# Four graph layers on one core: the product with v as one operation, the last residual by a transfer, the last five graphs' tiles turned by TensorE

## The chip, the cores and the metric

The kernel runs on one core of a Trainium2 chip. The metric is the time of one execution on the device in microseconds (us), the median of several runs. The engines are named as the profile names them: PE is TensorE's matrix product, PEld its loading of weights, DVE is VectorE, ACT is ScalarE, POOL is GpSimd, and SP is the engine that issues most transfers. PSUM, into which PE writes, is used as eight banks of 128 partitions by 2 KB.

## The reference

64 graphs of 256 nodes with 256 features each go through four layers; each layer's result is added to its input and normalized. All inputs are f32, `adj` is an integer matrix per graph.

```python
x = _layernorm(x + _L0_gnn_ref(x, adj, ...))   # attention with 8 heads of 32, then a feed-forward of 1024
x = _layernorm(x + _L1_gnn_ref(x, adj, ...))   # graph attention: leaky_relu(f_i + f_j), masked, softmax
x = _layernorm(x + _L2_gnn_ref(x, adj, ...))   # the same with another weight, then elu
x = _layernorm(x + _L3_gnn_ref(x, ..., adj, adj))  # two relational convolutions, each with elu
```

What matters here of layers 0 and 3, cut:

```python
# layer 0
scores = einsum('bhqd,bhkd->bhqk', q * scale, k)
attn = softmax(where(allowed, scores, -inf))
ctx = einsum('bhqk,bhkd->bhqd', attn, v)             # the product with v
# layer 3
def conv(x, w_rel, w_root, b):
    out = einsum('bnd,de->bne', x, w_root) + b
    for r in range(R):
        agg = einsum('bij,bid->bjd', masks[r], x) / deg[r]
        out = out + einsum('bjd,de->bje', agg, w_rel[r])
    return out
h = elu(conv(encoded_spans, w_rel1, w_root1, b1))
h = elu(conv(h, w_rel2, w_root2, b2))
return h                                              # then x + h, normalized: the last residual
```

## The kernel before

The kernel is unrolled over the 64 graphs. It first records every operation of every graph with its engine, a cost in microseconds that the author gave it, and the tiles that it reads and writes. A planner (`Plan.schedule`) then lays these operations out in time: on each engine it takes the ready operation that is due first, keeps PE in one mode of array tiling where it can, and gives out buffers from rings of fixed size. The instructions are emitted in that order, and each engine executes its own in order. So a change of one cost, tile or engine can move operations of all graphs.

```python
RINGS = {..., "p": 12, "both": 4, "inv": 1, "ctxT": 2, "X": 8, ..., "o": 4, "blocks": 1, "turned": 1, "xT": 2}
...
class Plan:
    LAG = {"PE": 0.21, "DVE": 0.13, "ACT": 0.13, "POOL": 0.08, "SP": 4.5}
    SWITCH = 0.1          # PE, on a change between "full", "row" and "col"
    PERIOD = 46.0         # a graph is due each 46 us
    LAST, SPACE = 5, 0.1  # the last five graphs are due nearly together
```

A graph has four tiles that must be transposed before they are multiplied with weights: the inputs of the two graph attention layers and of the two convolutions. They are turned through memory: DVE transposes blocks of 32x32, four transfers write the blocks in order to a buffer in HBM, and a fifth reads them back. `transposed` is the other way, used for the feed-forward: TensorE transposes into PSUM and ACT copies the result out.

```python
def transposed(xt):
    xT, pt = new("T", [P, KB, N]), new("bank", [P, KB, N])
    def issue():
        for kb in range(KB):
            for i in range(NB):
                nc.tensor.transpose(pt()[:, kb, i * P : (i + 1) * P], xt()[:, i, kb * P : (kb + 1) * P], ident)
    pe("full", 0.44, issue, [xt], [pt], [xT])
    act(0.47, lambda: nc.scalar.copy(xT(), pt()), [pt], [xT])
    return xT

def bounced(xt):
    turned, rows, xT = new("turned", [P, 4, NB * KB, 32]), new("rows", [P, NB * KB, 4, 32]), new("T", [P, NB * KB, P])
    dve(0.63, lambda: nc.vector.transpose(turned()..., xt()...), [xt], [turned], "uses")      # L629
    for a in range(4):
        op("SP", 0.5, lambda a=a: nc.sync.dma_start(rows()..., turned()...), [turned], [(rows, a)], lag=SENT)   # L633
    op("SP", 0.5, lambda: nc.sync.dma_start(xT()..., rows()...), [rows], [xT], lag=BACK)
    return xT, lambda kb, i: xT()[:, KB * i + kb, :]
```

With the planner's figures `SENT, BACK = 3.0, 4.5` for the time that these transfers take.

The product with v of the attention is done in two halves of four heads (`hg`). Each writes one PSUM bank: the sums of the exponentials and the unnormalized context. DVE takes the reciprocal of the sums and multiplies.

```python
inv = new("inv", [P, KB, N])
for hg in range(KB):
    pc = new("bank", [P, 2, N])
    def values(hg=hg, pc=pc):
        for r in range(4):
            nc.tensor.matmul(pc()[32 * r : 32 * r + 32, 1, :], lhsT=ones, rhs=both[r]()[:, hg, :], start=True, stop=True)   # L771
        for kt in range(NB):
            for r in range(4):
                h = 4 * hg + r
                nc.tensor.matmul(pc()[32 * r : 32 * r + 32, 0, :], lhsT=v()[:, kt, HD * h : HD * (h + 1)],
                                 rhs=p[kt, r]()[:, hg, :], start=(kt == 0), stop=(kt == NB - 1))                            # L776
    pe("col", 1.32, values, [v] + both + list(p.values()), [pc], [ctxT, inv])
    dve(1.62, lambda hg=hg, pc=pc: nc.vector.reciprocal(inv()[:, hg, :], pc()[:, 1, :]), [pc], [(inv, hg)])
    dve(0.28, lambda hg=hg, pc=pc: nc.vector.tensor_tensor(ctxT()[:, hg, :], pc()[:, 0, :], inv()[:, hg, :], op=ALU.mult), ...)
```

A residual is added in one of two ways. `add` is a DVE instruction. `add_later` is a transfer that GpSimd issues and that adds while it writes; so far it serves to add rows of constants to freshly loaded inputs.

```python
def add_later(xt, yt, reads):
    op("POOL", 0.6, lambda: nc.gpsimd.dma_start(xt(), yt(), accum_op=ALU.add), [xt, *reads], [xt], lag=3.0)   # L603
def add(xt, yt):
    dve(0.60, lambda: nc.vector.tensor_tensor(xt(), xt(), yt(), op=ALU.add), [xt, yt], [xt], "uses")          # L609
...
# end of each graph
h = conv(conv(xt, 0, rel, rdeg), 1, rel, rdeg)   # the result is a tile "o"
add(h, xt)                                       # the last residual
layer_norm(h)                                    # DVE statistics (L666, L668), POOL root (L671 to L674), ACT applies (L678)
op("SP", 0.4, lambda: nc.sync.dma_start(out_graph[g], h()), [h], [])
```

Of the kernel before, what the change touches and what calls it, by code (L numbers as in the profile page):

```python
# [17 lines left out]
P = 128  # L18
# [2 lines left out]
BIG = 1e30  # L21
NO_EDGE = -346.0


SENT, BACK = 3.0, 4.5

# [186 lines left out]
def tile_gnn_stack(ctx: ExitStack, tc: tile.TileContext, t: dict, out: bass.AP):  # L213
# [16 lines left out]
    nc = tc.nc  # L230
    x_in, adj_in = t["x"], t["adj"]
    B, N, D = x_in.shape
# [253 lines left out]
    def main_path(plan):  # L486
# [86 lines left out]
        def graph(g):  # L573
# [37 lines left out]
            def transposed(xt):  # L611
# [9 lines left out]
                act(0.47, lambda: nc.scalar.copy(xT(), pt()), [pt], [xT])  # L621
                return xT

            def bounced(xt):

                turned, rows, xT = new("turned", [P, 4, NB * KB, 32]), new("rows", [P, NB * KB, 4, 32]), new("T", [P, NB * KB, P])
                dve(0.63, lambda: nc.vector.transpose(turned().rearrange("p b q n -> p (b q n)"),  # L629
                                                      xt().rearrange("p i (k b c) -> p b (i k) c", k=KB, b=4)),  # L630
                    [xt], [turned], "uses")
                for a in range(4):
                    op("SP", 0.5, lambda a=a: nc.sync.dma_start(  # L633
                        rows().rearrange("(c b) q a n -> c (b q) a n", b=4)[:, :, a, :],
                        turned()[32 * a : 32 * a + 32].rearrange("c b q n -> c (b q) n")), [turned], [(rows, a)], lag=SENT)
                op("SP", 0.5, lambda: nc.sync.dma_start(xT().rearrange("p q n -> p (q n)"), rows().rearrange("p q a n -> p (q a n)")),
                   [rows], [xT], lag=BACK)
                return xT, lambda kb, i: xT()[:, KB * i + kb, :]
# [96 lines left out]
            def attention(xT, am):  # L735

                qk, v = projections(xT)
                ctxT = new("ctxT", [P, KB, N])  # L740
                p = {}
                for kt in range(NB):
                    s = [new("bank", [P, KB, N]) for r in range(4)]
                    for r in range(4):
                        p[kt, r] = new("p", [P, KB, N])

                    def scores(kt=kt, s=s):
                        for hg in range(KB):
                            for r in range(4):
                                f = slice(32 * r, 32 * r + 32)  # L750
                                nc.tensor.matmul(s[r]()[:, hg, :], lhsT=qk()[f, KB + hg, kt * P : (kt + 1) * P],  # L751
                                                 rhs=qk()[f, hg, :], start=True, stop=True)

                    pe("row", 0.97, scores, [qk], s, [p[kt, r] for r in range(4)])
                    for r in range(4):
                        pr, k = p[kt, r], 8 * g + 4 * kt + r
                        act(0.58, lambda pr=pr, k=k, sr=s[r]: nc.scalar.activation(  # L757
                            pr(), sr(), AF.Exp, accum_out=seen_sum[:, k : k + 1]), [s[r]], [pr])
                        dve(0.60, lambda pr=pr, kt=kt: nc.vector.tensor_tensor(  # L759
                            pr(), pr(), am()[:, kt, None, :].to_broadcast([P, KB, N]), op=ALU.mult), [pr, am], [pr], "uses")  # L760
                both = [new("both", [P, KB, N]) for r in range(4)]
                for r in range(4):
                    dve(0.60, lambda r=r: nc.vector.tensor_tensor(both[r](), p[0, r](), p[1, r](), op=ALU.add),  # L763
                        [p[0, r], p[1, r]], [both[r]], "uses")
                inv = new("inv", [P, KB, N])
                for hg in range(KB):
                    pc = new("bank", [P, 2, N])

                    def values(hg=hg, pc=pc):
                        for r in range(4):  # L770
                            nc.tensor.matmul(pc()[32 * r : 32 * r + 32, 1, :], lhsT=ones, rhs=both[r]()[:, hg, :],  # L771
                                             start=True, stop=True)
                        for kt in range(NB):
                            for r in range(4):
                                h = 4 * hg + r
                                nc.tensor.matmul(pc()[32 * r : 32 * r + 32, 0, :], lhsT=v()[:, kt, HD * h : HD * (h + 1)],  # L776
                                                 rhs=p[kt, r]()[:, hg, :], start=(kt == 0), stop=(kt == NB - 1))

                    pe("col", 1.32, values, [v] + both + list(p.values()), [pc], [ctxT, inv])
                    dve(1.62, lambda hg=hg, pc=pc: nc.vector.reciprocal(inv()[:, hg, :], pc()[:, 1, :]), [pc], [(inv, hg)])  # L780
                    dve(0.28, lambda hg=hg, pc=pc: nc.vector.tensor_tensor(
                        ctxT()[:, hg, :], pc()[:, 0, :], inv()[:, hg, :], op=ALU.mult), [pc, (inv, hg)], [(ctxT, hg)])
                act(0.62, lambda: nc.scalar.activation(inv(), inv(), AF.Identity, accum_out=seen_inv[:, g : g + 1]), [inv], [inv])  # L783
                return ctxT
# [32 lines left out]
                return y  # L817

            def gat(xt, layer, gm, seen, bias, finish):
                xT, xT_at = bounced(xt)  # L820
                w, c_w = gw[layer], c_gw[layer]
                h, e, z = new("h", [P, NB, HW]), tok("e"), tok("X")
                for i in range(NB):
                    ph = new("bank", [P, D + 2])
                    pe("full", 0.87, lambda i=i, ph=ph: product(ph(), lambda kb: xT_at(kb, i),
                                                                lambda kb: w[:, kb, :], KB), [xT, c_w], [ph], [h])
                    if bias is None:
                        act(0.27, lambda i=i, ph=ph: nc.scalar.copy(h()[:, i, 0 : D + 2], ph()), [ph], [(h, i)])
                    else:
                        dve(0.34, lambda i=i, ph=ph: nc.vector.tensor_tensor(h()[:, i, 0 : D + 2], ph(), bias, op=ALU.add),  # L830
                            [ph], [(h, i)])
                dve(0.07, lambda: nc.vector.memset(h()[:, :, ONE : ONE + 1], 1.0), [(h, 0), (h, 1)], [(h, "one")])
                dve(0.07, lambda: nc.vector.tensor_tensor(seen_fg[:, seen], h()[:, :, F_COL : G_COL + 1],
                                                          h()[:, :, F_COL : G_COL + 1], op=ALU.mult), [(h, 0), (h, 1)], [], "uses")
                pf = new("bank", [P, N])

                def spread():
                    for i in range(NB):
                        nc.tensor.transpose(pf()[:, i * P : (i + 1) * P],  # L839
                                            h()[:, i, F_COL : F_COL + 1].to_broadcast([P, P]), ident)  # L840

                pe("full", 0.22, spread, [(h, 0), (h, 1)], [pf], [e])
                for i in range(NB):
                    dve(0.40, lambda i=i: nc.vector.scalar_tensor_tensor(e()[:, i, :], pf(), h()[:, i, G_COL : G_COL + 1],  # L844
                                                                         gm()[:, i, :], op0=ALU.add, op1=ALU.min),
                        [pf, (h, i), gm], [(e, i)])
                dve(0.60, lambda: nc.vector.scalar_tensor_tensor(e(), e(), SLOPE, e(), op0=ALU.mult, op1=ALU.max), [e], [e],
                    "uses")
                act(0.52, lambda: nc.scalar.activation(e(), e(), AF.Exp), [e], [e])  # L849
                for i in range(NB):  # L850
                    po, r = new("bank", [P, HW]), new("r", [P, 1])
                    pe("full", 0.87, lambda i=i, po=po: product(po(), lambda kt: e()[:, kt, i * P : (i + 1) * P],
                                                                lambda kt: h()[:, kt, :], NB), [e, h], [po], [z, r])
                    dve(0.08, lambda po=po, r=r: nc.vector.reciprocal(r(), po()[:, ONE : ONE + 1]), [po], [r])
                    finish(i, z, po, r)
                return z
# [37 lines left out]
            def conv(h, layer, rel, rdeg):  # L894
# [1 line left out]


                w, c_w, bias = conv_w[layer], c_cw[layer], conv_b[layer]
                hT, hT_at = bounced(h)
                o, hi, lo, n = tok("o"), new("hi", [P, NB, D + 2], F32R), tok("lo", F32R), tok("e")  # L900
                cols = D if layer else D + 2
                for i in range(NB):
# [47 lines left out]
            rel = relation(load("adj", adj_graph[g], I32))  # L950
            rdeg = new("rdeg", [P, NB])
            h = conv(conv(xt, 0, rel, rdeg), 1, rel, rdeg)
            add(h, xt)
            layer_norm(h)
            op("SP", 0.4, lambda: nc.sync.dma_start(out_graph[g], h()), [h], [])

# [266 lines left out]
```

## Time and profile before

| What | Value |
|---|---|
| Time, median of 3 runs | 2896.01 us (2893.25 to 2898.55) |
| Span of the profiled execution | 2897.1 us |
| L609, DVE, last residual, 128x512 | 64 times, 682 ns each |
| L629, DVE, turning a tile, 128x512 | 256 times for these tiles, 702 to 703 ns each |
| Transfers rows<-turned, T<-rows | 1024 of 64 KB, 2.2 us from issue to landing; 256 of 256 KB, 2.8 us |
| L618, PE, one f32 transpose of 128x128 | 256 times, 277 ns each |
| L621, ACT, copy of 128x512 out of PSUM | 64 times, 588 ns each |
| L771 and L776, PE, product with v | 90.2 and 139.6 us busy |
| L603, POOL, issue of an adding transfer | 128 times, 1278 and 1301 ns each |

In the profile, `out<-in` are the tiles that an instruction writes and reads, by the names in the program. Many operations pass through helpers and so have the helper's line: L657 is the matrix product of every layer. "Idle before" is the time for which an engine stood still before an instruction, with the work that ended the wait. PE's busy time counts matmuls, whose ends are modelled. Time that an engine stands idle costs something only where it lies on the chain of work that sets the end.

### The profile page before, as it was taken

The page shows a single profiled execution, that of the slowest core. Times are in us where ns is not written, and L with a number is a line of the kernel's source. Part 1 is how long each engine was busy: PE and PEld are TensorE (multiplying, and loading weights), DVE is VectorE, ACT ScalarE, POOL GpSimd, SP SyncE. Part 2 cuts the span into 40 slices and gives each one's busy share as a digit, 9 for nine tenths or more (in the row PEclk, how much of TensorE's full clock was granted, in tenths as well). Part 3 has the DMA queues.
Part 4 walks back from the last instruction along what each step waited for, and adds up shares of the span by engine and source line. Part 5 has one row for each costly group of instructions (what it writes and reads, how often), then busy time and mean ns, then how long its engine had stood idle before and what let it go on. Part 6 is the DMA issues. An engine that isn't in the chain of part 4 may idle for free.

```text
span 2897.1 us, 50588 instructions
## 1 busy us (share of the span) xinstructions
PE 2805.3 (97%) x16182; PEld 2128.1 (73%) x16182; DVE 2523.0 (87%) x6557; ACT 1540.4 (53%) x3713; POOL 789.1 (27%) x1685
## 2 busy tenths in 40 slices
PE   8999999999999999999999999999999999999975
PEld 6776777777777767777777777777777777777853
DVE  6879899989989898999889898899888998999686
ACT  3555555546455555655555465555555655555343
POOL 2232223222223222222222322232231332222221
PEclk9999999999999999999999999999999999999998
DMA  7454455445444444454444544444444544443342
GB/s 183 81 108 88 99 101 102 89 101 102 95 92 100 87 94 94 98 101 93 104 97 93 98 99 99 100 91 102 86 93 96 109 88 93 105 90 72 67 83 70
DMA packets 844512, 278.32 MB, mean 96 GB/s; under 512 B 692656, under 2 KB 810672, under 8 KB 844240
## 3 DMA queue, kind: packets, MB, share of 16 engines
q1 hardware_dynamic: 808800, 240.27, 37.7%
q0 software_dynamic: 35440, 34.76, 8.5%
q8 instruction: 131, 2.15, 0.3%
q14 instruction: 141, 1.16, 0.1%
HBM read 157.43 MB, written 83.89 MB: 83 GB/s over the span
## 4 chain that ended last, share of the span: by engine, by line
PE 82%; DVE 10%; ACT 3%; DMA 2%; issue 2%; POOL 1%; SPq 1%; DVEq 0%; POOLq 0%; ACTq 0%
PE bank L657 67%; PE bank L919 4%; PE bank L776 3%; PE bank L751 3%; PE bank L771 2%; DMA rows<-turned 2%; DVE p L759 1%; PE bank L618 1%; DVE turned L629 1%; PE bank L839 1%; SPq L633 1%; DVE st L666 1%; DVE o L929 1%; DVE both L763 1%; DVE e L844 1%
## 5 line engine op out<-in xcount | busy, mean ns | idle before, releaser
L671 POOL TENSOR_SCALAR rstd<-mv 128x2 f32<-128x2 f32 x384 | 104.4, 272 | 1869.8 <-DVE mv L668 1496.7
L678 ACT ACTIVATE X<-X,rstd 128x256 f32<-128x256 f32 x640 | 349.8, 597 | 244.7 <-POOL rstd L674 230.1
L657 PE MATMUL bank<-cw,T 128*128 128x512 f32 x1024 | 467.9, 600 | 9.6 <-DMA T<-rows 9.1
L657 PE MATMUL bank<-T,w 128*128 128x256 f32 x2048 | 471.6, 380 | 5.2 <-ACT p L757 2.6
L657 PE MATMUL bank<-w,hid 128*128 128x256 f32 x2048 | 460.1, 380 | 0.0
L657 PEld LDWEIGHTS bank<-w,hid 128*128 128x128 f32 x2048 | 385.9, 190 | 62.7 <-issue 10.4
L657 PEld LDWEIGHTS bank<-T,w 128*128 128x128 f32 x2048 | 382.7, 190 | 64.5 <-issue 6.9
L757 ACT ACTIVATE p<-bank 128x512 f32<-128x512 f32 x512 | 299.9, 598 | 87.8 <-PE bank L751 87.6
L657 PEld LDWEIGHTS bank<-cw,T 128*128 128x128 f32 x1024 | 192.2, 192 | 209.3 <-issue 195.2
L759 DVE TENSOR_TENSOR p<-p,am 128x512 f32<-128x512 f32 x512 | 332.8, 680 | 10.8 <-ACT p L757 10.7
L672 POOL TENSOR_TENSOR rstd<-rstd,neghalf 128x2 f32<-128x2 f32 x384 | 305.7, 796 | 32.1
L809 ACT ACTIVATE hid<-bank,col_b 128x256 f32<-128x256 f32 x512 | 209.4, 474 | 113.8 <-PE bank L657 112.1
L657 PE MATMUL bank<-xT,wqkv 128*128 128x256 f32 x1024 | 251.6, 387 | 13.4 <-DVE xT L650 12.9
L657 PE MATMUL bank<-h,e 128*128 128x259 f32 x1024 | 253.8, 388 | 11.0 <-ACT e L849 9.3
L657 PE MATMUL bank<-gw,T 128*128 128x258 f32 x1024 | 249.1, 384 | 2.1 <-ACT inv L783 1.5
L657 PEld LDWEIGHTS bank<-h,e 128*128 128x128 f32 x1024 | 192.7, 192 | 66.6 <-issue 19.3
L666 DVE BATCH_NORM_STATS2 st<-X 128x6 f32<-128x256 f32 x640 | 237.5, 413 | 1.8
L906 ACT CAST hi<-bank 128x256 fp32r<-128x256 f32 x256 | 94.6, 370 | 263.4 <-PE bank L657 262.6
L657 PEld LDWEIGHTS bank<-xT,wqkv 128*128 128x128 f32 x1024 | 189.7, 192 | 54.0 <-issue 13.5
L780 DVE RECIPROCAL inv<-bank 128x256 f32<-128x256 f32 x128 | 220.0, 1734 | 8.8 <-PE bank L776 8.6
L657 PEld LDWEIGHTS bank<-gw,T 128*128 128x128 f32 x1024 | 191.1, 191 | 36.7 <-issue 5.2
L629 DVE STREAM_TRANSPOSE turned<-X 128x512 f32<-128x512 f32 x192 | 134.9, 703 | 45.0 <-DMA rows<-turned 23.0
(121 smaller groups left out, 4775.4 us busy)
## 6 DMA issues: line engine op xcount, KB each, us to landing
rows<-turned SPq DMA_DIRECT2D x1024, 64.0 KB, 2.2
T<-rows SPq DMA_DIRECT2D x256, 256.0 KB, 2.8
adj<-in_adj_dram SPq DMA_DIRECT2D x128, 256.0 KB, 3.0
blocks<-in_x_dram SPq DMA_DIRECT2D x512, 32.0 KB, 2.3
x<-in_x_dram SPq DMA_DIRECT2D x64, 256.0 KB, 3.0
xr<-in_x_dram SPq DMA_DIRECT2D x64, 256.0 KB, 2.8
xr<-row_ln_b POOLq DMA_DIRECT2D x64, 256.0 KB, 4.4
x<-row_bo POOLq DMA_DIRECT2D x64, 256.0 KB, 4.8
```

The lines of the kernel that those rows point to most:

```text
L629: dve(0.63, lambda: nc.vector.transpose(turned().rearrange("p b q n -> p (b q n)"), xt().rearrange("p i (k b c) -> p b (i k) c", k=KB, b=4 ...
L657: nc.tensor.matmul(dst, lhsT=lhs(c), rhs=rhs(c), start=(c == 0), stop=(c == n - 1))
L666: nc.vector.bn_stats(stat()[:, i, :], y()[:, i, :])
L671: nc.gpsimd.tensor_scalar(rstd()[:, 0, :], mv()[:, :, 1], 1.0, EPS, op0=ALU.mult, op1=ALU.add)
L672: nc.gpsimd.tensor_tensor(rstd()[:, 0, :], rstd()[:, 0, :], neghalf[:, 0:NB], op=ALU.pow)
L678: nc.scalar.activation(y()[:, i, :], y()[:, i, :], AF.Identity, bias=rstd()[:, 1, i : i + 1], scale=rstd()[:, 0, i : i + 1])
L757: act(0.58, lambda pr=pr, k=k, sr=s[r]: nc.scalar.activation(pr(), sr(), AF.Exp, accum_out=seen_sum[:, k : k + 1]), [s[r]], [pr])
L759: dve(0.60, lambda pr=pr, kt=kt: nc.vector.tensor_tensor(pr(), pr(), am()[:, kt, None, :].to_broadcast([P, KB, N]), op=ALU.mult), [pr, am] ...
L780: dve(1.62, lambda hg=hg, pc=pc: nc.vector.reciprocal(inv()[:, hg, :], pc()[:, 1, :]), [pc], [(inv, hg)])
L809: act(0.36, lambda f=f, k=k, ph=ph: nc.scalar.activation(hid()[:, f + k, :], ph()[:, k, :], AF.Relu, bias=b1[:, f + k : f + k + 1]), [ph, ...
L906: act(0.27, lambda i=i, po=po: nc.scalar.copy(hi()[:, i, 0:D], po()[:, D:]), [po], [(hi, i)])
L919: nc.tensor.matmul(pa()[:, 0:n], lhsT=rel()[:, i, j * P : (j + 1) * P], rhs=part()[:, i, 0:n], start=(c == 0), stop=(c == len(terms) - 1))
```

## The change

Three things are changed. The two halves of the product with v become one operation of the planner, which writes two banks. The last residual is added by a transfer for all graphs but the last two. For the last five graphs (`QUICK`) the four tiles are transposed by TensorE instead of through memory: ACT first copies the tile with its columns rearranged, so that the result has the order of rows that the weights are laid out for. The first is to keep the planner from parting the two halves, the second to take work off DVE, the third to shorten the end, where there are no later graphs to work on meanwhile.

```diff
+QUICK = 5
...
+            def rearranged(xt):
+                if g < B - QUICK:
+                    return bounced(xt)
+                spread = tok("turned")
+                act(0.8, lambda: nc.scalar.copy(spread().rearrange("p i (k c b) -> p (i k) c b", k=KB, b=4),
+                                                xt().rearrange("p i (k b c) -> p (i k) c b", k=KB, b=4)), [xt], [spread])
+                xT = transposed(spread)
+                return xT, lambda kb, i: xT()[:, kb, i * P : (i + 1) * P]
...
                 inv = new("inv", [P, KB, N])
-                for hg in range(KB):
-                    pc = new("bank", [P, 2, N])
-
-                    def values(hg=hg, pc=pc):
+                pcs = [new("bank", [P, 2, N]) for hg in range(KB)]
+
+                def values():
+                    for hg in range(KB):
+                        pc = pcs[hg]()
                         for r in range(4):
...   (the same products, with pc for pc())
-                    pe("col", 1.32, values, [v] + both + list(p.values()), [pc], [ctxT, inv])
+                pe("col", 2.62, values, [v] + both + list(p.values()), pcs, [ctxT, inv])
+                for hg in range(KB):
+                    pc = pcs[hg]
                     dve(1.62, lambda hg=hg, pc=pc: nc.vector.reciprocal(inv()[:, hg, :], pc()[:, 1, :]), [pc], [(inv, hg)])
...
             def gat(xt, layer, gm, seen, bias, finish):
-                xT, xT_at = bounced(xt)
+                xT, xT_at = rearranged(xt)
...   (in conv)
-                hT, hT_at = bounced(h)
+                hT, hT_at = rearranged(h)
...
             h = conv(conv(xt, 0, rel, rdeg), 1, rel, rdeg)
-            add(h, xt)
+            if g < B - 2:
+                add_later(h, xt, [xt])
+            else:
+                add(h, xt)
             layer_norm(h)
```

More of the change, by code (lines that the diff above doesn't have):

```diff
@@ L765, in attention @@
                 inv = new("inv", [P, KB, N])
-                for hg in range(KB):
-                    pc = new("bank", [P, 2, N])
-                    def values(hg=hg, pc=pc):
+                pcs = [new("bank", [P, 2, N]) for hg in range(KB)]
+                def values():
+                    for hg in range(KB):
+                        pc = pcs[hg]()
                         for r in range(4):
-                            nc.tensor.matmul(pc()[32 * r : 32 * r + 32, 1, :], lhsT=ones, rhs=both[r]()[:, hg, :],
+                            nc.tensor.matmul(pc[32 * r : 32 * r + 32, 1, :], lhsT=ones, rhs=both[r]()[:, hg, :],
                                              start=True, stop=True)
@@ L775, in values @@
                                 h = 4 * hg + r
-                                nc.tensor.matmul(pc()[32 * r : 32 * r + 32, 0, :], lhsT=v()[:, kt, HD * h : HD * (h + 1)],
+                                nc.tensor.matmul(pc[32 * r : 32 * r + 32, 0, :], lhsT=v()[:, kt, HD * h : HD * (h + 1)],
                                                  rhs=p[kt, r]()[:, hg, :], start=(kt == 0), stop=(kt == NB - 1))
-                    pe("col", 1.32, values, [v] + both + list(p.values()), [pc], [ctxT, inv])
+                pe("col", 2.62, values, [v] + both + list(p.values()), pcs, [ctxT, inv])
+                for hg in range(KB):
+                    pc = pcs[hg]
                     dve(1.62, lambda hg=hg, pc=pc: nc.vector.reciprocal(inv()[:, hg, :], pc()[:, 1, :]), [pc], [(inv, hg)])
```

## The prediction

> **What bounds the kernel now.** I read the page first (busy times, the span in 40 slices), then busy times by stretch, then the chain that ended last and the waits, both cut to the last 164 us.
>
> The page, engine shares and slices:
>
> ```profile
> PE 2805.3 (97%) x16182; PEld 2128.1 (73%) x16182; DVE 2523.0 (87%) x6557; ACT 1540.4 (53%) x3713; POOL 789.1 (27%) x1685
> ...
> PE   8999999999999999999999999999999999999975
> ...
> DVE  6879899989989898999889898899888998999686
> ...
> PEclk9999999999999999999999999999999999999998
> ```
>
> PE is full in every slice but the first and the last two. DVE is near full too, but with gaps. A number by stretch says more (columns: stretch, its length, busy us and instructions of PE, weight loads, DVE, ACT and POOL, granted clock, DMA share, GB/s):
>
> ```profile
> 40.00:300.00 260.00, 257.36 (x1588) 199.16 (x1587) 224.87 (x558) 140.15 (x352) 67.00 (x142) 1.00 0.50 101
> ...
> 2400.00:2700.00 300.00, 299.16 (x1813) 227.35 (x1812) 273.31 (x683) 168.05 (x414) 76.66 (x174) 1.00 0.42 87
> 2700.00:2733.00 33.00, 33.00 (x157) 29.01 (x156) 15.70 (x41) 12.99 (x30) 8.44 (x19) 1.00 0.33 67
> 2733.00:2780.00 47.00, 37.95 (x166) 30.39 (x165) 37.77 (x123) 17.85 (x37) 13.87 (x35) 0.96 0.40 76
> 2780.00:2840.00 60.00, 48.06 (x161) 28.40 (x160) 48.75 (x158) 24.60 (x53) 10.11 (x28) 0.91 0.44 90
> 2840.00:2897.00 57.00, 30.10 (x94) 15.41 (x92) 31.43 (x89) 19.71 (x38) 6.70 (x20) 0.83 0.25 62
> ```
>
> There are two regimes. From 40 to 2700 us PE is busy 2630 of 2660 us; the nine stretches that I asked for leave it 29.8 us idle together. Nothing done to another engine can bring more than those 29.8 us there. From 2733 us to the end, 164 us, PE is busy 116 us and DVE 118 us: neither is full, and what sets the pace is latency from one engine to the next. In that tail the last graphs have no later graph to hide behind. The chain of work that ended last says the same; its shares by line for 2733 to 2897 us:
>
> ```profile
> by line: PE bank L657 21.3%; issue 6.5%; DMA rows<-turned 6.5%; DVE e L844 4.4%; DVE turned L629 4.4%; DMA T<-rows 4.2%; SPq L633 3.9%; DVE o L929 3.2%; ACT e L934 3.1%; PE bank L919 2.9%; DVE st L666 2.9%; DVE lo L907 2.8%; DVE e L847 2.8%
> ```
>
> The turn of a tile through memory (DVE turned, the issues at SPq L633, both DMAs) is 4.4 + 3.9 + 6.5 + 4.2 = 19.0% of it, 31 us. DVE's turns in this tail are 20, 14 of X and 6 of o; five graphs have 15 and 5, so all but one or two are those of the last five graphs. The timeline of the last one: DVE starts to turn at 2869.97, the product that needs it starts at 2877.73, 7.8 us later. Another, from 2843.47 to 2852.81, took 9.3 us.
>
> **What the Trainium skill says.** "VectorE: DVE Perf Modes", section "The three transpose paths": DVE transposes 32x32 blocks only, TensorE a whole 128x128 into PSUM. That fits this trace: DVE's turn takes 0.70 us and then five transfers have to put the blocks in place. "TensorE: Matmul & The Clock Gate", "Part 4: PE-mode transpose", adds that the result needs a copy out of PSUM; the trace has both, 277 ns for an f32 transpose (L618) and 588 ns for ACT's copy (L621). The same page, "What's actually happening" under the clock gate, says that a TensorE idle for a window of some 3.4 us falls to half clock. The tail agrees: granted clock 0.83 in its last stretch, and the eight products of 128x512 at 2852.81, after 3.05 us of waiting for T<-rows, took 5.37 us where the same eight at 2859.92 took 3.60. "DMA: Bandwidth & Descriptors", "Anatomy of one DMA", puts a transfer from GpSimd at 2.0 us + bytes / 436e3, an estimate of 2.6 us for 256 KB. The trace gives 4.4 and 4.8 us from issue to landing for the same form (xr<-row_ln_b, x<-row_bo), of which 1.26 us is the issuing instruction. The measurement decides.
>
> **Part 1, both halves of the product with v in one operation.** No instruction is added or taken away. The two halves are a burst of 4 + 8 products each, for groups of 32 columns. In the built order before, all 64 graphs already have the two bursts one after the other, with nothing between; so it is after. No change of mode is saved: I count 367 changes before, 371 after. What it changes is planning: two PSUM banks are claimed at once, and the planner lets the first reciprocal (DVE, 1.73 us) follow both bursts instead of the first. On a PE that is full anyway I put this at 0 us.
>
> **Part 2, the last residual by transfer, 62 of 64 graphs.** DVE loses 62 x 0.682 us (row X+o, L609) = 42 us, of its 2523. POOL gains 62 issues x 1.26 us = 78 us on 789. The new wait is at DVE's statistics of o: they cannot start before the sum has landed. The planner believes in 0.6 + 3.0 = 3.6 us for issue and transfer; the rows above measured 4.4 to 4.8. I added up, in the order as built, the DVE work placed between each transfer and its statistics, with the durations of the profile's rows: 4.2 us in the median, 3.8 to 4.5 between the quartiles, 1.2 the least. So DVE, which keeps its order, stands still some 0.2 to 0.6 us in most graphs, 12 to 37 us in all, against 42 us of work saved: about even for DVE, and DVE does not set the end before 2733. For PE I take 0.
>
> **Part 3, the last five graphs turned by TensorE.** Each of 20 turns loses 0.70 us of DVE and five transfers, and gains an ACT copy that rearranges (like other ACT passes over 128x512 from SBUF, 0.63 to 0.72 us), four transposes (0.44 us for the group at 2699.94), and ACT's copy (0.59). With three handovers of 0.05 to 0.2 us that is some 2.1 us in place of 7.8: 5.7 saved per turn on the path. DVE loses 14 us in the tail, ACT gains 20 x 1.3 = 26 on 62, PE 20 x 0.5 = 10 on 116; none gets full by this. On the chain lie 31 / 7.8 = 4 turns, as one would expect of one graph with its two attention layers and two convolutions. So 31 - 4 x 2.1 = 22.6 us leave this chain. Other graphs' chains stand just behind it, waiting for DVE and PE in turn; I let them take back a third and keep 15. The warmer clock may add a little: the 96 products of 128x512 in the tail average 647 ns against 600 over all, 4.5 us, of which I count 1.
>
> **Sum.** Start 0, full stretch 0, tail -16: 2896 - 16 = 2880 us.
>
> **The rivals.** (a) A reshuffle of the full stretch. Parts 1 and 2 alter what the planner sees, and its order changes from the first graphs on: hardly a stretch of PE's order is the same, and from a few graphs on the new order repeats every seven graphs, which the old did not. If that pattern has a place where PE waits, it waits there in every repetition. The stretches before range from 0.5 to 6.3 us of idle per 300, so one like the best all along gives about 20 us more (2860), one with twice the idle costs 30 (2910). Nothing in the profile tells which; it is the largest uncertainty. (b) The transfer stalls DVE more than worked out, because the POOL queue, which waits for o in its order, also holds up the roots of other norms (each waits 1.26 us for an issue where 0.6 was planned), and ACT's longest waits are for just those (L678, 230 us in all). Then DVE and ACT come late by 1 to 2 us per graph. Against it: only 10% of DVE's time is free but PE waits little for DVE now, a few us per line. If a quarter of 62 x 1.5 us reached PE it would be +23: about 2903. (c) The tail's gain is taken back whole, as its other limit is DVE with 118 of 164 us and queues on it: 2896. For this: the chain in the tail also runs through dozens of short DVE pieces. Against it: DVE itself loses 14 us there. (d) All of the 22 us and a warmer clock are kept, and the full stretch loses half its idle: 2858.
>
> **Range and chances.** The tail gives 5 to 25, the full stretch anything from -20 to +20: 2860 to 2902 for 8 times in 10. Two per cent is 58 us; to be under 2838 the kernel would have to lose nearly all idle time of the full stretch and half of the tail's, to be over 2954 it would need about three times the idle of now. Faster by over 2%: 0.03; within: 0.94; slower: 0.03.
>
> **What would show it.** Right: no DVE turned and no rows<-turned in the last 150 us, the stretch after PE ceases to be full some 15 us shorter, clock there at 0.9 or more; DVE about 2470 us busy, with short new waits of st (L666) on the transfer o<-X of 0.2 to 0.6 us each; PE some 2810 us busy, idle between 40 and 2700 us near 30. Wrong: PE idle there of over 45 us with releasers on DVE or POOL (a or b); a tail as long as before with DVE over 80% busy in it (c); or a landing of o<-X well above 4.8 us.

## The result

| | Time, median | Ratio to the kernel before |
|---|---|---|
| Before | 2897.01 us (2893.25 to 2898.55) | |
| Changed | 2866.45 us (2865.78 to 2867.83) | 0.9897 (95% interval 0.9880 to 0.9914) |

The gain is 30 us, within two per cent and within the range that was given, and about twice the 16 us that the sum expected. For experiments the ratio is given with its 95% interval, and "us" is the ratio's distance from 1 times 2897 us.

### The profile page after: what moved, and what is told of

It reads as the page before. It is cut to its first block, busy times and chain, and to the rows that moved or that the text cites. A ratio compares the mean times of both kernels' runs of the same rounds, so it can differ in the third digit from the quotient of the medians.

```text
span 2864.0 us, 50548 instructions
## 1 busy us (share of the span) xinstructions
PE 2799.7 (98%) x16262; PEld 2130.6 (74%) x16262; DVE 2479.8 (87%) x6475; ACT 1563.8 (55%) x3753; POOL 847.5 (30%) x1747
## 3 DMA queue, kind: packets, MB, share of 16 engines
q14 instruction: 139, 1.14, 0.1%
## 4 chain that ended last, share of the span: by engine, by line
PE 72%; DVE 13%; DMA 7%; ACT 2%; issue 2%; SPq 2%; POOL 1%; DVEq 0%; POOLq 0%; ACTq 0%
PE bank L669 59%; DMA o<-X 3%; PE bank L934 3%; PE bank L789 3%; PE bank L763 3%; DMA rows<-turned 2%; DVE p L771 2%; PE bank L784 2%; DVE st L678 1%; SPq L645 1%; DVE turned L641 1%; DVE o L944 1%; PE bank L854 1%; DVE inv L795 1%; PE bank L620 1%
## 5 line engine op out<-in xcount | busy, mean ns | idle before, releaser
L669 PE MATMUL bank<-T,w 128*128 128x256 f32 x2048 | 473.2, 380 | 0.6 <-ACT T L623 0.3
L669 PE MATMUL bank<-cw,T 128*128 128x512 f32 x1024 | 462.7, 595 | 0.6 <-ACT T L623 0.6
L669 PE MATMUL bank<-w,hid 128*128 128x256 f32 x2048 | 459.4, 380 | 0.0
L669 PEld LDWEIGHTS bank<-T,w 128*128 128x128 f32 x2048 | 381.3, 190 | 64.7 <-issue 12.4
L669 PEld LDWEIGHTS bank<-w,hid 128*128 128x128 f32 x2048 | 385.4, 190 | 58.1 <-issue 4.3
L769 ACT ACTIVATE p<-bank 128x512 f32<-128x512 f32 x512 | 299.0, 597 | 75.2 <-PE bank L763 75.1
L669 PEld LDWEIGHTS bank<-cw,T 128*128 128x128 f32 x1024 | 191.5, 190 | 198.9 <-issue 182.0
L669 PE MATMUL bank<-xT,wqkv 128*128 128x256 f32 x1024 | 249.5, 386 | 12.3 <-DVE xT L662 12.3
L669 PE MATMUL bank<-h,e 128*128 128x259 f32 x1024 | 252.2, 386 | 7.4 <-ACT e L864 5.7
L669 PE MATMUL bank<-gw,T 128*128 128x258 f32 x1024 | 249.9, 385 | 7.2 <-DMA T<-rows 2.6
L669 PEld LDWEIGHTS bank<-h,e 128*128 128x128 f32 x1024 | 192.2, 191 | 66.8 <-issue 21.6
L669 PEld LDWEIGHTS bank<-xT,wqkv 128*128 128x128 f32 x1024 | 188.7, 191 | 53.8 <-issue 17.7
L669 PEld LDWEIGHTS bank<-gw,T 128*128 128x128 f32 x1024 | 191.3, 191 | 43.2 <-issue 10.0
L864 ACT ACTIVATE e<-e 128x512 f32<-128x512 f32 x128 | 80.7, 631 | 169.9 <-DVE e L862 169.2
```

The lines of the kernel that those rows point to most:

```text
L669: nc.tensor.matmul(dst, lhsT=lhs(c), rhs=rhs(c), start=(c == 0), stop=(c == n - 1))
L769: act(0.58, lambda pr=pr, k=k, sr=s[r]: nc.scalar.activation(pr(), sr(), AF.Exp, accum_out=seen_sum[:, k : k + 1]), [s[r]], [pr])
```

## The profile after

The page of the changed kernel, engine shares and two of the slices:

```profile
PE 2799.7 (98%) x16262; PEld 2130.6 (74%) x16262; DVE 2479.8 (87%) x6475; ACT 1563.8 (55%) x3753; POOL 847.5 (30%) x1747
...
PE   8999999999999999999999999999999999999987
...
PEclk9999999999999999999999999999999999999999
```

DVE has 82 instructions fewer (62 additions, 20 turns). Their groups are 42.2 and 13.5 us less busy, the 56 us worked out, but the engine as a whole only 43: instructions in a row overlap a little (in the timeline three of 0.68 us take 1.89), and such time counts once. POOL gained 58 us for 62 issues. PE is the surprise: 80 instructions more for the transposes, 12.8 us of busy time, yet 5.6 us less busy in all. The product with v is 6.5 us less busy (85.4 + 137.9 us, before 90.2 + 139.6) and the 128x512 products 5.2; why is not shown. Busy times by stretch (columns as before):

```profile
40.00:2700.00 2660.00, 2635.93 (x15489) 2010.01 (x15489) 2345.63 (x6057) 1453.74 (x3541) 794.28 (x1625) 1.00 0.50 102
...
2733.00:2780.00 47.00, 37.80 (x169) 29.29 (x168) 36.58 (x128) 30.93 (x57) 12.46 (x36) 0.93 0.11 23
2780.00:2820.00 40.00, 38.22 (x163) 24.98 (x162) 32.73 (x114) 28.00 (x53) 6.15 (x16) 1.00 0.10 21
2820.00:2864.00 44.00, 27.74 (x110) 15.79 (x108) 28.47 (x87) 25.72 (x47) 10.91 (x26) 0.90 0.21 56
```

PE is idle 24.1 us between 40 and 2700 us, where it was 29.8. From 2733 us on there are 131 us left instead of 164, with PE busy 104 of them (79%) instead of 116 (71%). The chain that ended last, 2733 to 2864 us:

```profile
by line: PE bank L669 42.8%; DMA o<-X 5.1%; PE bank L934 4.4%; ACT turned L631 4.1%; ACT X L690 4.0%; issue 3.9%; PE bank L620 3.9%; DVE o L950 2.8%; DMA rows<-turned 2.5%; DVE st L678 2.3%; ACT e L949 2.2%; DVE o L944 1.9%; ACT e L948 1.7%
```

Products (L669, before L657) hold 43% of the end's chain, before 21%; of the turn through memory 2.5% of a transfer is left, from an earlier graph. In its place stand ACT's rearranging copy (L631) and the transposes (L620). One whole turn, from the timeline (start, duration, engine, line):

```profile
2797.43 1.12 ACT L631 COPY turned<-o 128x512 f32<-128x512 f32 x1
...
2798.97 0.60 PE L620 MATMUL bank<-ident,turned 128*128 128x128 f32 x4
...
2800.67 0.59 ACT L623 COPY T<-bank 128x512 f32<-128x512 f32 x1
...
2801.32 1.98 PE L669 MATMUL bank<-cw,T 128*128 128x512 f32 x4
```

3.9 us from the start of the copy to the product, 1.1 of them because ACT copied another tile before it took the result out. The last turn of the kernel has nothing in between; its product starts at 2845.94, 2.5 us after the copy:

```profile
2843.43 1.12 ACT L631 COPY turned<-o 128x512 f32<-128x512 f32 x1 [0.41 <-DVE o L950]
...
2844.61 0.65 PE L620 MATMUL bank<-ident,turned 128*128 128x128 f32 x4
...
2845.30 0.59 ACT L623 COPY T<-bank 128x512 f32<-128x512 f32 x1 [0.74 <-PE bank L620]
```

Read in this way from the trace, the 20 turns take 2.5 to 33 us, 5.4 in the median. The 20 last turns through memory, before, take 7.6 to 11.9 us, 8.7 in the median.

What PE itself waited for from 2733 us on (us in all, times, longest), first before, then changed:

```profile
PE bank L657 <- DMA T<-rows: 9.4, 3, 5.7
PE bank L919 <- DVE hi L912: 7.5, 5, 2.4
PE bank L657 <- ACT e L849: 7.4, 5, 2.2
PE bank L919 <- DVE lo L907: 5.9, 8, 1.7
...
PE bank L620 <- ACT turned L631: 6.1, 5, 3.6
PE bank L934 <- DVE lo L922: 2.9, 3, 1.2
PE bank L669 <- ACT T L623: 2.8, 4, 1.1
PE bank L669 <- ACT e L864: 1.5, 2, 1.3
```

PE waits for the turns themselves hardly less: 9.4 us for T<-rows before, 6.1 + 2.8 for the copies now. What went are waits for other work of the last graphs, on DVE (hi, lo) and ACT (e), 20.8 us before and 5.0 now. In e1, part 3 alone, it is the same: 10.4 us for the turns and 4.6 for these. A likely reading is that tiles that arrive sooner let the work of one graph fill the waits of another. But DVE also has 18 turns fewer in this stretch, some 12.7 us, and these are the waits that it could shorten. No run here separates the two.

And the new wait of part 2, DVE's statistics behind the transfer (us in all, times, longest):

```profile
DVE st L678 <- DMA o<-X: 58.0, 45, 5.2
```

**An account.** PE bounds the kernel, so the span is PE's busy time plus its idle time, which I split at 40 and 2700 us. One profiled execution each. e1, e6 and e9, whose order is that of the kernel before up to 2400 us at least, differ from it by 2.6, 3.4 and 0.8 us in the column for 40 to 2700, so differences up to some 3 us there mean nothing.

| Kernel | Span | PE busy | Idle to 40 | Idle 40 to 2700 | Idle from 2700 |
|---|---|---|---|---|---|
| before | 2897.1 | 2805.3 | 14.0 | 29.8 | 48.0 |
| changed | 2864.0 | 2799.7 | 13.0 | 24.1 | 27.2 |
| e1, part 3 alone | 2881.2 | 2806.5 | 14.5 | 32.4 | 27.7 |
| e2, part 2 alone | 2907.9 | 2809.8 | 17.4 | 34.4 | 46.3 |
| e3, part 1 alone | 2892.2 | 2805.0 | 16.2 | 29.7 | 41.3 |
| e4, parts 1 and 2 | 2887.9 | 2800.8 | 15.8 | 25.6 | 45.6 |
| e5, transfer replaced in place | 2860.5 | 2799.8 | 16.8 | 15.8 | 28.0 |
| e6, period 46.5 | 2890.7 | 2802.6 | 13.9 | 33.2 | 41.0 |
| e7, reciprocal 1.73 | 2924.9 | 2818.1 | 16.7 | 42.6 | 47.5 |
| e8, measured figures | 2878.7 | 2803.2 | 17.0 | 28.7 | 29.8 |
| e9, PE kept warm | 2903.0 | 2816.6 | 16.3 | 30.6 | 39.5 |
| e10, last 2 turned | 2873.7 | 2798.8 | 18.1 | 26.2 | 30.5 |
| e11, last 8 turned | 2867.9 | 2805.7 | 15.8 | 23.2 | 23.2 |
| e12, e5 with last 8 | 2855.7 | 2802.2 | 14.8 | 16.7 | 22.0 |

The last column sorts the kernels: 22 to 31 us wherever TensorE turns the last tiles, 39 to 48 us wherever they go through memory. Within a group it moves with order alone: by 7 us in e6, which has the instructions of the kernel before. PE's busy time ranges from 2799 to 2818 us for nearly the same products. The mean granted clock differs too (0.991 before, 0.996 changed, 0.988 in e7); how much of the range it explains is not separated.

## The experiments: each part by itself

My theory after the result: the shorter end is the gain, and the rest is another order of the full stretch. The rival: the other two parts do the work, by relieving DVE or by keeping the halves of the product together.

**e1_turn_only.** Part 3 alone; the first 85% of PE's order is word for word that of the kernel before.

```diff
-            if g < B - 2: add_later(h, xt, [xt]) ...
+            add(h, xt)                       # and the product with v in two operations again
```

> Only the last five graphs are turned by TensorE; the product with v and the last residual are as before. Each engine's order is that of the kernel before up to where the last graphs begin (PE's first 2412 of 2840 rows are the same). Theory A, the gain is the shorter end (turns 5 us shorter each, PE's clock no longer falling): 2896 - 25 = about 2871, PE idle from 40 to 2700 us as before (near 30 us). Rival B, the gain comes from the other two parts (DVE relieved, another order in the full stretch) and the end gives little: 2885 to 2893.

Measured: 0.9932 (0.9919 to 0.9946), -20 us. PE's idle time from 2700 us falls from 48.0 to 27.7 us. The middle, with the old order, does not gain:

```profile
40.00:2700.00 2660.00, 2627.59 (x15417) 2001.05 (x15416) 2366.11 (x6096) 1453.36 (x3528) 732.98 (x1557) 1.00 0.47 96
```

Two thirds of the gain is the end. It is somewhat less than the 25 us expected.

**e2_add_only.** Part 2 alone: `QUICK = 0`, product with v in two operations.

> Only the last residual goes by a transfer. Theory A: within 8 us of the kernel before (2888 to 2904), as PE is full where DVE is relieved. Rival B, DVE's 42 us less work let PE wait less: 2875 to 2886. Rival C, DVE's wait for the transfer reaches PE: over 2905.

Measured: 1.0035 (1.0022 to 1.0047), +10 us: slower, though DVE has 30 us less to do (2493.2 us busy). Rival B falls for this order, and theory A's 8 us is exceeded. PE's idle time to 2700 us is 8.0 us more than before, and PE is 4.5 us longer busy; the longest waits of PE in that stretch are for ACT (e L861 7.1 us, p L769 6.2 us), not directly for the statistics behind the transfer. C's number came, and its cause may be part of it: PE's wait for ACT's e is one that shrinks in e5 when the transfer is taken out. How much of the 10 us is order stays open.

**e3_values_only.** Part 1 alone: `QUICK = 0`, `add(h, xt)` for all graphs.

> Only the two halves of the product with v are one operation of the planner. No instruction is added or taken away, only the order changes. Theory A: any difference is that of another order, within 8 us of the kernel before. Rival D, keeping the halves in one operation is itself what makes the full stretch denser: 2880 to 2888, and parts 1 and 2 together no better than this.

Measured: 0.9966 (0.9954 to 0.9978), -10 us, a little more than theory A's 8. The middle is not denser (29.7 us idle against 29.8); what shrank is the idle time of the end, 41.3 against 48.0. Rival D named the full stretch, so it falls; whether the operation as such helps cannot be told from this run.

**e4_no_turn.** Parts 1 and 2: `QUICK = 0` and nothing else.

> Parts 1 and 2 without the turning by TensorE: the changed kernel's order up to row 2439 of PE's 2835, then an end with turns through memory. Theory A: 25 us above the changed kernel, about 2890, with the last stretch after PE ceases to be full as long as in the kernel before. Rival B: about 2872, within 8 us of the changed kernel.

Measured: 0.9976 (0.9964 to 0.9987), -7 us. Turning by TensorE on top of it is worth 0.9976 - 0.9897, 23 us. The end keeps its idle time (45.6 us). Note that parts 1 and 2 do not add up: -10 and +10 alone, -7 together. Two savings of work should add up; two orders need not. That led to the next runs.

## The experiments: work saved or order

**e5_same_order.** The order of the changed kernel is kept, but a DVE addition stands in the transfer's place.

```diff
-                add_later(h, xt, [xt])
+                op("POOL", 0.6, lambda: nc.vector.tensor_tensor(h(), h(), xt(), op=ALU.add), [h, xt], [h], lag=3.0)
```

> The changed kernel with its planned order kept: the planner still sees the last residual as a transfer of GpSimd, but in its place in the order stands a DVE addition. PE and ACT have the changed kernel's order without any difference. DVE has 42 us more work, and its 58 us of waiting for the transfers are gone. Theory A, part 2 acts through the order that the planner makes of it and not through relief of DVE: within 5 us of the changed kernel (0.988 to 0.992 of the kernel before). Rival B, the relief of DVE is what lets PE run on: 10 us or more above the changed kernel (ratio 0.993 or more). Rival C, the wait for the transfer costs: 5 us or more below it.

Measured: 0.9894 (0.9879 to 0.9909), -31 us, against 0.9897 for the changed kernel: the same within the intervals. DVE is busy 2513.6 us instead of 2479.8, and its 58 us of waiting for the transfer are gone. Its longest waits now:

```profile
DVE X L807 <- PE bank L669: 101.6, 53, 5.3
DVE lo L922 <- ACT hi L921: 41.9, 65, 2.3
```

DVE waits 9 us more for PE (101.6 us, in the changed kernel 92.2) and works 34 us more, and the time does not rise. So the gain of the changed kernel does not rest on relief of DVE; nearly all that part 2 brings is the order that the planner makes when it believes in it.

The transfer does cost PE something, though. The full stretch of e5, and PE's wait there for ACT's L864 in the changed kernel and in e5:

```profile
40.00:2700.00 2660.00, 2644.22 (x15530) 2016.65 (x15529) 2381.88 (x6128) 1461.43 (x3555) 746.53 (x1569) 1.00 0.47 96
...
PE bank L669 <- ACT e L864: 4.2, 6, 1.0
...
PE bank L669 <- ACT e L864: 0.7, 1, 0.7
```

PE idles 15.8 us where it idled 24.1 with the transfer. Up to 2400 us the order of PE and ACT is the same in six of the kernels. PE idles there, from 40 us on, 22.8 us (changed), 21.3 (e4), 21.9 (e10) and 22.9 (e11) with the transfer, 14.4 (e5) and 14.8 (e12) without: 7 to 8 us. The time shows little of it, 1 us here and 5 us between e11 and e12, both within the intervals; PE's idle time before 40 us alone differs by 3.8 us between the profiled executions of e5 and of the changed kernel. The swap takes away DVE's relief and its waits at once, so what either does alone is not shown.

**e6_period and e7_reciprocal.** The kernel before with one of the planner's own figures changed. The instructions are the same, only their order differs: for e6 late (PE's from row 2503 of 2820), for e7 almost from the start.

```diff
-    PERIOD = 46.0
+    PERIOD = 46.5          # e6
-    dve(1.62, ... reciprocal ...)
+    dve(1.73, ... reciprocal ...)   # e7
```

> The kernel before, with the planner's period of 46.0 us per graph set to 46.5 and nothing else: the same instructions, in another order near the end (PE's first 2503 of 2820 rows are the same). Theory A, an order alone moves the end by several us: between 2885 and 2910, not within 2 us. Rival: the order matters little at this level, within 2 us of the kernel before, so that the differences of parts 1 and 2 need another cause.

> The kernel before, with the planner told that the reciprocal takes 1.73 us (as the profile measured) in place of 1.62: the same instructions, in another order from the first graphs on. Theory A: the time moves by 3 to 12 us in either direction, as much as part 1 or part 2 alone did (-8.7 and +10.4). Rival: within 3 us.

Measured: e6 0.9975 (0.9968 to 0.9982), -7 us; e7 1.0103 (1.0087 to 1.0118), +30 us. An order alone, with not one instruction changed, moves the time over a span of 37 us, more than e2, e3 and e4 did, and further than I had expected (3 to 12 us). e7's figure is the truer one, the duration in the profile, and it gave the slowest kernel of all. Its full stretch:

```profile
40.00:2700.00 2660.00, 2617.36 (x15275) 1987.94 (x15274) 2359.28 (x6057) 1440.49 (x3506) 730.58 (x1534) 0.99 0.47 96
```

42.6 us idle, 13 more than before. The idle time after 2700 us is as before (47.5). The rest of the longer span is 13 us more of busy PE time and 3 us at the start.

**e8_true_figures.** The changed kernel with the planner told what the profile measured for the new operations.

```diff
-    op("POOL", 0.6, ... accum_op=ALU.add ..., lag=3.0)    act(0.8, ... spread ...)
+    op("POOL", 0.9, ... accum_op=ALU.add ..., lag=3.6)    act(1.1, ... spread ...)
```

> The changed kernel with the planner told what the profile measured for the new operations: 0.9 us for the issue of the residual's transfer and 3.6 us until its sum can be read (before 0.6 and 3.0), 1.1 us for ACT's rearranging copy (before 0.8). Theory A: DVE's waits for the transfer (58 us) nearly go, yet the time stays within 8 us of the changed kernel, as PE did not wait for them. Rival C, these waits reach PE: 8 to 20 us below the changed kernel.

Measured: 0.9955 (0.9942 to 0.9969), -13 us, which is 17 us slower than the changed kernel. DVE's wait for the transfer fell from 58.0 to 9.5 us, as meant, and the kernel got slower: neither expectation held. The end is short as in all kernels that turn by TensorE (29.8 us idle); the difference lies before 2700 us (8.7 us more idle) and in 3.5 us of busy time. It is one more order, no measure of the wait.

## The experiments: what makes the end shorter

**e9_warm.** Is it latency, or that PE's clock falls in the waits? The kernel before, with two spare products ahead of the first product of a turned tile in the last five graphs; their results are overwritten at once.

```diff
+            def warm(bank, i):
+                if g >= B - 5 and i == 0:
+                    for _ in range(2):
+                        nc.tensor.matmul(bank[:, 0:D], lhsT=ident, rhs=wo[:, 0, :], start=True, stop=True)
```

> The kernel before (turns through memory), with two products of 128x256 added to PE before the first product that needs a turned tile, in the last five graphs: 20 times, results overwritten at once, no other change of any order. They can run while PE waits for T<-rows and keep it active. If the falling clock is a large part of what the shorter turns save: clock in the last 160 us at 0.95 or more and 3 to 8 us below the kernel before. Rival, it is the latency alone: no faster, 0 to 10 us slower for 20 x 0.9 us of added work that partly lies in idle time.

Measured: 1.0027 (1.0013 to 1.0040), +8 us. The 128x512 products of the end, before and here, and the spare ones, from 2733 us on (times, busy us, mean ns):

```profile
L657 PE MATMUL bank<-cw,T 128*128 128x512 f32 x96 | 48.0, 647 | 8.8 <-DMA T<-rows 8.8
...
L662 PE MATMUL bank<-cw,T 128*128 128x512 f32 x96 | 44.9, 612 | 4.3 <-DMA T<-rows 4.3
...
L657 PE MATMUL bank<-wo,ident 128*128 128x256 f32 x76 | 21.2, 405 | 0.0
```

The clock did respond: the mean fell from 647 to 612 ns, and the granted clock from 2780 to 2840 us rose from 0.91 to 0.97. But at 0.87 in the last stretch it missed the 0.95 that I had asked for, and the 21 us of spare products cost more than this saved. The clock alone is thus not shown to bring time; how much of the 20 us is latency, how much the clock and how much DVE's fewer turns stays open. An upper bound for the 128x512 products comes from the changed kernel, where their mean in the end is 596 ns: 96 x 51 ns = 4.9 us. The other products of the end, scaled to equal counts, are busy another 4.7 us less there, an estimate from their groups in the two traces, of which the clock may again be a part.

**e10_quick2 and e11_quick8.** `QUICK = 2` and `QUICK = 8` in the changed kernel.

> The changed kernel with only the last two graphs turned by TensorE. Theory A, each turn saved on the chain of the last graph is what counts: as the last graph has four turns in either case, most of the 20 us stays: 3 to 10 us above the changed kernel. Rival, the turns of all five graphs count as they run into one another: 12 us or more above, at 2878 or more where the kernel before has 2897.

> The changed kernel with the last eight graphs turned by TensorE. Theory A: the three further graphs are turned where PE is full, so 12 x 0.5 us of transposes are added to PE and nothing saved: 3 to 8 us above the changed kernel. Rival, the end starts earlier than I read it and they help: below the changed kernel by over 2 us.

Measured: e10 0.9918 (0.9904 to 0.9931), -24 us; e11 0.9883 (0.9868 to 0.9898), -34 us. Of the 23 us that turning gives over e4, the last two graphs alone bring 17 (0.9976 - 0.9918), which fits a chain on which one graph's four turns lie. With eight graphs the interval overlaps that of five. In the profile PE is 5.9 us longer busy and 4.0 us less idle in the end; but the profiled execution was the slowest of its four (2869.71 us, median 2864.16) and had a mean clock of 0.994 where the others had 0.996, so not all of the 5.9 us need be the extra transposes. Theory A's 3 to 8 us above the changed kernel did not come; whether eight beats five is not settled.

**e12_both.** e5 with `QUICK = 8`.

> The changed kernel's order with the DVE addition in the transfer's place, and the last eight graphs turned by TensorE: the two single edits that came out no slower than the changed kernel (2865 and 2864 us). If each is worth what its median said, 2861 to 2864 (ratio 0.987 to 0.989); if both were noise about the changed kernel, 0.9885 to 0.991.

Measured: 2858.18 us, 0.9867 (0.9850 to 0.9883), -39 us: the fastest of all kernels here, beyond what either expectation said in the median. Its interval just overlaps that of the changed kernel (from 0.9880), so the 9 us between them are likely, not proved. It has no transfer for the last residual, and against e11, which has it, it is 5 us faster by the ratios, again within the intervals: the transfer is at best not needed.

## Why the prediction was right, and where not

- **What bounds it.** Two regimes, PE full up to about 2733 us and latency after: held. e5 shows it most sharply: DVE is 34 us longer busy, and no time is lost.
- **Part 3, -16 us.** Right that the end gets shorter, and a little low: -20 alone (e1), -23 on top of parts 1 and 2. On the way there, terms were off in opposite directions, so that the number is near is in part luck. A turn was put at 2.1 us; with nothing in between it takes 2.5, as the rearranging copy takes 1.1 us where I had 0.63 to 0.72 from plain passes of the same size. In the end as it runs it takes 5.4 us in the median against 8.7 before, since ACT and PE do other work in between, so a turn saves rather 3.3 us than 5.7. And "let them take back a third" was too cautious: the idle time in the end fell by 20.3 us in e1, near the 22.6 of the chain alone. It did not fall in PE's waits for the turns, 9.4 us before and 8.9 in the changed kernel, but in those for DVE and ACT; how much of that is the shorter turn and how much DVE's 18 turns fewer stays open. The clock term, put at 1 us, stays open, up to 4.9 us for the 128x512 products. Rival (c), that the end gives nothing, fell.
- **Part 1 and part 2, 0 each.** That a full PE gains nothing from relief of DVE: e5 agrees. As a sum, wrong by -7 us (e4), and by the size that rival (a), another order, had been given: 20 us faster to 30 us slower. e6 and e7 (-7 and +30) lie within it, e7 at its edge. The new order does repeat, though every six graphs (600 instructions of DVE in the trace) and not every seven, and a wait in it recurs: transfers issued at 1436.6, 1698.7, 1962.1 and 2224.2 us ended in DVE waits of 3.8, 5.2, 3.7 and 2.9 us. Rival (b), that the transfer's stall reaches PE, is there but small: 7 to 8 us of idle time in the full stretch (e5), where (b) had 23 and the sum 0.
- **The transfer.** Issue 0.91 us and 4.0 us from issue to landing in the median, both below the 1.26 and 4.4 to 4.8 that I took from the broadcast form. Still DVE waited 58 us in 45 graphs, 1.3 each, not 0.2 to 0.6: a median says little where the landing has a long tail. It goes up to 7.6 us, and that transfer gave the longest wait, 5.2 us.
- **The signs named.** PE idle near 30 in the full stretch (24.1), clock at 0.9 or more, DVE near 2470 us (2479.8): seen. "No DVE turned in the last 150 us" was not: three turns of graphs ahead of the last five still run there.

## What to carry to other kernels

In a kernel that a planner or scheduler lays out, change one of its figures without touching the work, and see how far the time moves; here that was 37 us, so a gain of 10 us from a real change says nothing about its mechanism. To separate work from order, keep the order and swap only the instruction, as in e5, and read the idle time of the engine that sets the pace beside the total: it showed a cost of 7 to 8 us that the total hid. Where one engine is full, look for gains in its idle time alone: that of the end, where nothing is left to hide latency behind, was the one that could be had for a reason.

## What was not expected of the hardware

- ACT's copy of 128x512 f32 from SBUF that rearranges columns (it reads single elements 32 apart, and writes them one after the other) took 1.06 to 1.14 us, against 0.63 us for a plain pass of the same size (L864).
- An adding transfer of 256 KB from a full tile took 0.91 us to issue and 4.0 us to land, against 1.28 to 1.31 us and 4.3 to 4.7 us in the same run from a row repeated in the source.
- Products spread over the idle times of PE, 0.9 us each turn, raised the granted clock in 60 us of the end from 0.91 to 0.97.
